# A dilation stage whose next rows are loaded ahead of the last rows' store and used one call later, and one PSUM bank copied by ScalarE

## The chip, the core and the metric

The kernel runs on one core of one Trainium2 chip. The metric is the device time of one launch in microseconds. Engines are named as the profile names them: PE is TensorE (PEld its weight loads), DVE is VectorE, ACT is ScalarE, POOL is GpSimd and SP is SyncE; the last two issue DMAs here and compute almost nothing. [...]

## What is computed

The input is 8 images of 8 channels of 256 x 256 in float32. Layer 0 of the reference is a Fourier operator (four rounds of spectral convolution plus 1x1 convolution, then a 1x1 convolution to 512 channels and one back to 8). Layer 1 is a dilation by a 3 x 3 square, padded by -2, of the normalized result. Both are added to their input:

```python
x = x + _L0_conv_ref(_gn(x), ...)
x = x + _L1_conv_ref(_gn(x))          # 3x3 maximum, border -2
```

## The kernel before, in words

**Three images are in work at once.** While image b goes through its four spectral layers (`layers`, L703), the two fully connected convolutions of image b-1 (its *head*, L789) are woven between them, and the dilation of image b-2 (its *tail*, `dilate`, L871) between those. The order on PE, DVE, ACT and SP is written out by hand: every stage is a generator that yields a string at the places where it lets others in. The loop at L938 reads the string: `f` is one step of the first convolution of a head (L825: 8 matmuls into four PSUM banks, then `act` by ACT at L826 and L827), `c` or `C` one of the second (L842: 16 matmuls, then a DVE addition at L851), and `t` one *call* of the oldest tail, that is, the dilation's code up to its next `yield`.

**A layer** handles the image in 11 chunks, two by two (k = 0 to 5). For each chunk `burst` (L593) makes 48 matmuls into four PSUM banks (L603 or L600, L606), which ACT evicts to `h` (L611, in layer 3 L613); DVE transposes the chunk in `turn` (L550); `transform` (L557) multiplies two chunks (L567) and DVE and ACT evict that (L574, L575); `gather` (L577) multiplies again (L585) and DVE evicts to `zt` (L588, L591). Where a pair has both chunks, k = 2 to 4 yields `ft`, then runs turn and transform, yields `t`, runs the second burst, yields `t`, and ends with `fc`. The last, single chunk (k = 5) yields `f`, then one `t`, then `fc`. Layer 3 has none of the turning; it yields `fct` eight times.

**Between two layers** stand the spectrum (`spectrum_h`, L375), the mixing on DVE (`mix`, L412) and, for the even layers, `rows_even` (L483). That one multiplies in three groups (`oi` = 0, 1, 2; L496) into PSUM banks `p_g`; group 0 has four banks, one in a buffer of one bank (`one`) and three in a buffer of three (`tri`), the other groups have three. There are two buffers of each kind, handed round in turn by all stages. `copy_banks` (L210) copies the banks to `zt`, by ACT (L215) those whose places are named in its second argument, by DVE (L217) the rest. In group 0 the banks are taken in the order 1, 2, 3, 0: the three of `tri` first. After image 0 (`alone[0]` false) groups 0 and 1 are copied by DVE alone, and of group 2 two banks by ACT.

**The dilation** of one image goes over 16 rows per partition in 8 groups of two rows. `yin` (one buffer, two rows and a row above and below), `m` and `o` (one buffer each) serve all groups. One group takes five calls:

- the last call of the group before ends with the store of `o` (L906) and, after the loop's turn, the load of `yin` (L878, 512 KB), both issued by POOL;
- a call that does nothing;
- the call that makes `m`, the maximum of neighbours (L889);
- the call that finishes it (L891), then the one that makes `o` (L894, L895);
- the call that normalizes `o`, sets the border and adds `yin` (L898 to L905), and then stores and loads as above.

The store waits for the addition L905; so does the load, which overwrites `yin`. `dilate` serves images 0 to 6; image 7 has its own stage (L747).

Of the kernel before, what the change touches and what calls it, by code (L numbers as in the profile page):

```python
# [39 lines left out]
DR = 2  # L40
# [6 lines left out]
def fno_dilate_kernel(ctx: ExitStack, tc: tile.TileContext, a: dict, out: bass.AP):  # L47
# [14 lines left out]
    def ps_tri(name):  # L62
        return ps.tile([128, 3, 512], F32, tag="tri", bufs=2, name=name)

    def ps_four(name):
        one, tri = ps_a(f"{name}_0"), ps_tri(f"{name}_1")
        return one, tri, [one] + [tri[:, i, :] for i in range(3)]

    def part(i):
        return slice(32 * i, 32 * i + 32)  # L70
# [137 lines left out]
    alone = [True]  # L208

    def copy_banks(pairs, by_act):  # L210

        done = []
        for i, (dst, src) in enumerate(pairs):
            if i in by_act:
                ins = nc.scalar.activation(dst, src, AF.Identity).ins  # L215
            else:
                ins = nc.vector.tensor_copy(dst, src).ins  # L217
            for other in done:
                if other.engine != ins.engine:
                    tc.declare_no_dep(ins, other, reason="two engines read banks of one tile and write apart")  # L220
            done.append(ins)
# [7 lines left out]
    def stats_end(st, name, out_):  # L229
        mv = sb.tile([128, 2], F32, tag="mv", name=f"mv_{name}")  # L230
        nc.vector.bn_aggr(mv, st.rearrange("p n s -> p (n s)"))
        yield
        yield
        p = corner(f"p_st_{name}")
        mm(p, grp, mv[:, 0:1], start=True, stop=True)
        if guest[0] is not None:
            yield
        mr = sb.tile([128, 2], F32, tag="mr", bufs=4, name=f"mr_{name}")
        nc.vector.tensor_copy(mr[:, 0:1], p)
        d = sb.tile([128, 1], F32, tag="d", name=f"d_{name}")  # L240
        nc.vector.tensor_tensor(d, mv[:, 0:1], mr[:, 0:1], ALU.subtract)
        nc.vector.scalar_tensor_tensor(mv[:, 1:2], d, d, mv[:, 1:2], ALU.mult, ALU.add)
        yield
        yield
        q = corner(f"p_sv_{name}")
        mm(q, grp, mv[:, 1:2], start=True, stop=True)
        if guest[0] is not None:
            yield


        v, r = mv[:, 0:1], mr[:, 1:2]
        nc.vector.tensor_scalar(v, q, EPS, None, ALU.add)
        rsqrt(v, r, d)
        yield
        out_["mr"] = mr
# [227 lines left out]
    def rows_even(b, l):  # L483

        zv = zt[:, :, :, : NBLK * WID].rearrange("p r f (n o) -> p o n f r", n=NBLK)
        n = NBLK * CS * NQ
        yield "ffc"
        for oi in range(NO):
            name = f"p_g_{b}_{l}_{oi}"
            if oi == 0:  # L490
                one, tri, banks = ps_four(name)
            else:
                tri = ps_tri(name)
                banks = [tri[:, r, :] for r in range(3)]
            for r, p in enumerate(banks):
                mm(p[:, :n], fz[part(r), oi].rearrange("p g k -> p (g k)"),  # L496
                   rowg[part(r), :, r % 2, :], start=True, stop=True)
            pairs = [(zv[:, NO * r + oi], banks[r][:, :n].rearrange("p (f n r) -> p n f r", n=NBLK, r=CS))
                     for r in ((1, 2, 3, 0) if oi == 0 else (0, 1, 2))]
            copy_banks(pairs, (0, 2) if oi == 2 else (1, 3) if alone[0] else ())  # L500
            yield "fcf"[oi]
        if l < 3:
            yield "t"
# [182 lines left out]
    def start(b, out_):  # L686
        if b < n_img:
            if b == 0:
                out_["sw"] = [load_sw(0, k) for k in range(3)]
            yield from spectrum_x(b, out_)  # L690
            yield from mix(b, 0, out_)
# [11 lines left out]
    def layers(b, stored, d, then, ahead):  # L703

        for l in range(4):
            if l > 0:
                yield from spectrum_h(b, l, d)  # L710
                yield from mix(b, l, d)
            yield from rows_odd(b, l, then) if l % 2 else rows_even(b, l)
            yield from layer(b, l, d, stored, then, ahead)
        yield "stored"
        yield from rest(b, then)
# [152 lines left out]
        return done, first, second, ahead  # L868


    def dilate(b, stats):  # L871
        d = {}
        yield from stats_end(stats, f"y{b}", d)
        mr = d["mr"]
        whole = y_rows[b % 2][:]
        o_rows = out[b].rearrange("c (p f) -> (c p) f", p=16)
        for r in range(0, 16, DR):
            nc.gpsimd.dma_start(  # L878
                yin[:, :, 1 : HW + 1],
                bass.AP(whole.tensor, whole.offset + r * HW, [[16 * HW, 128], [HW, DR + 2], [1, HW]]))  # L880
            yield
            yield

            if r == 0:
                nc.vector.tensor_scalar(yin[:, 0, :], yin[:, 0, :], edge[:, 0:1], None, ALU.min)
            if r == 16 - DR:
                nc.vector.tensor_scalar(yin[:, DR + 1, :], yin[:, DR + 1, :], edge[:, 1:2], None, ALU.min)
            m = sb.tile([128, DR + 2, HW], F32, tag="m", bufs=1, name=f"m_{b}_{r}")
            nc.vector.tensor_tensor(m, yin[:, :, 0:HW], yin[:, :, 1 : HW + 1], ALU.max)  # L889
            yield  # L890
            nc.vector.tensor_tensor(m, m, yin[:, :, 2 : HW + 2], ALU.max)  # L891
            yield
            o = sb.tile([128, DR, HW], F32, tag="o", bufs=1, name=f"o_{b}_{r}")
            nc.vector.tensor_tensor(o, m[:, 0:DR], m[:, 1 : DR + 1], ALU.max)  # L894
            nc.vector.tensor_tensor(o, o, m[:, 2 : DR + 2], ALU.max)  # L895
            yield

            nc.vector.tensor_scalar(o, o, mr[:, 0:1], mr[:, 1:2], ALU.subtract, ALU.mult)  # L898
            nc.vector.tensor_scalar(o[:, :, 0:1], o[:, :, 0:1], PAD, None, ALU.max)
            nc.vector.tensor_scalar(o[:, :, HW - 1 : HW], o[:, :, HW - 1 : HW], PAD, None, ALU.max)  # L900
            if r == 0:
                nc.vector.tensor_scalar(o[:, 0, :], o[:, 0, :], edge[:, 2:3], None, ALU.max)
            if r == 16 - DR:
                nc.vector.tensor_scalar(o[:, DR - 1, :], o[:, DR - 1, :], edge[:, 3:4], None, ALU.max)
            nc.vector.tensor_tensor(o, o, yin[:, 1 : DR + 1, 1 : HW + 1], ALU.add)  # L905
            nc.gpsimd.dma_start(o_rows[:, HW * r : HW * (r + DR)], o.rearrange("p r w -> p (r w)"))  # L906


# [17 lines left out]
    def tail():  # L926
        if tails and next(tails[0], tails) is tails:
            tails.pop(0)

    stats_of = {}  # L930
    with tc.manual_schedule(engines={PE, DVE, ACT, SP}):
        d = {}
        for _ in start(0, d):
            pass
        for b in range(n_img):
            stored = [dram.tile([128, NQ * PIX], F32, tag=f"hs{c}", name=f"stored_{b}_{c}") for c in range(NCH)]
            nxt, new, n_ready = {}, None, 0
            for n in layers(b, stored, d, start(b + 1, nxt), nxt):  # L938
                if n == "ready":
                    if new is None:  # L940
                        if b + 1 < n_img:
                            stats_of[b] = sb.tile([128, 8, 6], F32, tag="bn_y", name=f"bn_y{b}")
                        else:
                            stats_of[b] = spare[:, 16384:16480].rearrange("p (n s) -> p n s", s=6)
                        new = head(b, stored, stats_of[b])
                    new[3](n_ready)
                    n_ready += 1
                elif n == "stored":
                    heads.append((b, new))
                    alone[0] = False  # L950
                else:
                    for kind in n or "":
                        if kind == "t":
                            tail()
                        elif heads:
                            step(kind)
            d = nxt
        while heads:
            for kind in "ffc":
                if heads:  # L960
                    step(kind)
            tail()
        for t in tails:
            for _ in t:
                pass
# [170 lines left out]
```

## Time and profile before

| | |
|---|---|
| median of 3 runs | 3673.78 us (3665.64 to 3674.04) |
| the profiled execution | 3669.94 us, its span 3668.1 us |
| PE busy | 3478.0 us, 95% of the span |
| ACT busy | 2865.8 us, 78% |
| DVE busy | 2388.5 us, 65% |
| DVE waiting for `yin` before L889 | 26.1 us in 12 of 56 groups |
| mean granted PE clock | 0.979 |

Two views are read in what follows. The timeline shows instructions in order of time: start, duration, engine, line and operation, then in brackets how long the engine stood idle before it and what ended that. The list of waits adds these idle times up: who waited for whom, microseconds in all, how often, and the longest. Busy time is the sum over the whole span; PE's matmuls are pipelined, so 95% busy doesn't mean that 95% of the time PE could not have been faster.

### The profile page before, as it was taken

The page shows a single profiled execution, that of the slowest core. Times are in us where ns is not written, and L with a number is a line of the kernel's source. Part 1 is how long each engine was busy: PE and PEld are TensorE (multiplying, and loading weights), DVE is VectorE, ACT ScalarE, POOL GpSimd, SP SyncE. Part 2 cuts the span into 40 slices and gives each one's busy share as a digit, 9 for nine tenths or more (in the row PEclk, how much of TensorE's full clock was granted, in tenths as well). Part 3 has the DMA queues.
Part 4 walks back from the last instruction along what each step waited for, and adds up shares of the span by engine and source line. Part 5 has one row for each costly group of instructions (what it writes and reads, how often), then busy time and mean ns, then how long its engine had stood idle before and what let it go on. Part 6 is the DMA issues. An engine that isn't in the chain of part 4 may idle for free.

```text
span 3668.1 us, 112640 instructions
## 1 busy us (share of the span) xinstructions
PE 3478.0 (95%) x50872; PEld 1269.3 (35%) x50872; DVE 2388.5 (65%) x3711; ACT 2865.8 (78%) x3021; POOL 117.0 (3%) x202
## 2 busy tenths in 40 slices
PE   5768999999999999999999999999999999999997
PEld 2323333333333333333333333333333333333222
DVE  6776666557775677756776577766777567772443
ACT  2435888888788888787888888888878888879986
POOL 1000000000000000000000000000000000000000
PEclk7879999999999999999999999999999999999998
DMA  3006111442225312271214512253222531225221
GB/s 92 16 16 213 50 50 47 154 119 72 71 87 191 86 52 66 91 223 56 67 56 136 170 56 78 61 174 110 73 72 84 192 85 54 64 70 190 85 81 48
DMA packets 114081, 344.71 MB, mean 94 GB/s; under 512 B 15985, under 2 KB 18481, under 8 KB 98177
## 3 DMA queue, kind: packets, MB, share of 16 engines
q1 hardware_dynamic: 95392, 276.32, 24.8%
q0 software_dynamic: 18208, 61.18, 5.1%
q8 instruction: 400, 6.55, 0.7%
q14 instruction: 81, 0.66, 0.1%
HBM read 213.44 MB, written 123.74 MB: 92 GB/s over the span
## 4 chain that ended last, share of the span: by engine, by line
PE 74%; DVE 15%; issue 5%; ACT 4%; DMA 2%; POOL 0%; ACTq 0%; DVEq 0%; POOLq 0%
PE p_fc L842 20%; PE p_fc L825 20%; PE p_z L606 9%; PE p_d L567 7%; PE p_z L603 7%; PE p_z L600 3%; DVE turned L550 3%; PE p_u L585 3%; DVE y L851 3%; DVE S L423 2%; DVE turned L420 2%; DMA yin<-y_rows 2%; DVE turned L381 1%; PE p_g L518 1%; PE p_b L390 1%
## 5 line engine op out<-in xcount | busy, mean ns | idle before, releaser
L827 ACT ACTIVATE act<-p_fc 128x1536 f32<-128x1536 f32 x1024 | 1493.0, 1458 | 3.1 <-PE p_fc L825 3.1
L825 PE MATMUL p_fc<-hs,c_w 32*128 32x512 f32 x8192 | 1133.3, 626 | 29.8 <-DVE y L851 10.0
L842 PE MATMUL p_fc<-act,c_w 128*32 128x512 f32 x8192 | 1007.5, 599 | 0.2 <-ACT act L827 0.2
L826 ACT ACTIVATE act<-p_fc 128x512 f32<-128x512 f32 x1024 | 616.3, 602 | 214.1 <-PE p_fc L825 201.5
L550 DVE STREAM_TRANSPOSE turned<-h 128x1024 f32<-128x1024 f32 x528 | 632.4, 1225 | 179.0 <-ACT h L611 178.4
L611 ACT ACTIVATE h<-p_z 128x512 f32<-128x512 f32 (+1 forms) x528 | 511.9, 1021 | 205.0 <-PE p_z L606 204.9
L851 DVE TENSOR_TENSOR y<-p_fc,y 128x512 f32<-128x512 f32 x392 | 267.9, 683 | 524.9 <-PE p_fc L842 524.9
L825 PEld LDWEIGHTS p_fc<-hs,c_w 32*128 32x128 f32 x8192 | 356.6, 183 | 602.0 <-ACT act L826 259.2
L842 PEld LDWEIGHTS p_fc<-act,c_w 128*32 128x32 f32 x8192 | 222.5, 109 | 704.7 <-issue 330.7
L606 PE MATMUL p_z<-c_binv,zt 32*128 32x256 f32 x5632 | 410.4, 405 | 0.0
L606 PEld LDWEIGHTS p_z<-c_binv,zt 32*128 32x128 f32 x5632 | 259.3, 186 | 307.5 <-issue 294.4
L603 PE MATMUL p_z<-h,c_wt 32*32 32x512 f32 x8448 | 357.0, 602 | 7.9 <-ACT act L826 4.2
L567 PE MATMUL p_d<-turned,c_fw 32*32 32x480 f32 (+1 forms) x9216 | 308.9, 541 | 0.7 <-DVE turned L550 0.4
L575 ACT ACTIVATE turned<-p_d 128x1440 f32<-128x1440 f32 x144 | 182.9, 1270 | 90.9 <-PE p_d L567 87.6
L613 ACT ACTIVATE h<-p_z,c_bias 128x512 f32<-128x512 f32 (+1 forms) x176 | 186.5, 1110 | 71.7 <-PE p_z L606 71.5
L215 ACT ACTIVATE zt<-p_g 128x198 f32<-128x198 f32 (+2 forms) x118 | 53.6, 576 | 182.1 <-PE p_g L496 98.4
L423 DVE TENSOR_REDUCE S<-turned 128x80 f32<-128x800 f32 x192 | 189.0, 984 | 5.9
L420 DVE TENSOR_TENSOR turned<-t,B 128x800 f32<-128x800 f32 x192 | 188.7, 983 | 1.1
L567 PEld LDWEIGHTS p_d<-turned,c_fw 32*32 32x32 f32 x9216 | 127.3, 103 | 166.0 <-issue 65.0
L381 DVE STREAM_TRANSPOSE turned<-zt 128x960 f32<-128x960 f32 x96 | 177.2, 1873 | 2.5
L603 PEld LDWEIGHTS p_z<-h,c_wt 32*32 32x32 f32 x8448 | 93.2, 103 | 174.4 <-DVE y L851 48.8
L585 PE MATMUL p_u<-turned,c_stack 128*32 128x480 f32 (+1 forms) x1152 | 136.7, 543 | 11.5 <-DVE turned L574 6.2
(198 smaller groups left out, 1754.1 us busy)
## 6 DMA issues: line engine op xcount, KB each, us to landing
stored<-h SPq DMA_DIRECT2D x88, 1024.0 KB
hs<-stored SPq DMA_DIRECT2D x352, 256.0 KB
t<-in_spw SPq DMA_DIRECT2D x96, 400.0 KB
yin<-y_rows POOLq DMA_DIRECT2D x56, 512.0 KB, 5.1
h<-in_xp SPq DMA_DIRECT2D x352, 48.0 KB
turned<-in_xw SPq DMA_DIRECT2D x16, 1024.0 KB
y<-in_x SPq DMA_DIRECT2D x56, 256.0 KB
y_rows<-y POOLq DMA_DIRECT2D x56, 256.0 KB, 4.1
```

What stands on the lines that cost most here:

```text
L420: nc.vector.tensor_tensor(pr, sw[k], bt[:, k2, k].unsqueeze(2).to_broadcast([128, G, 2 * WID, WID]), ALU.mult)
L423: nc.vector.tensor_reduce(s[k2][:, k].rearrange("p s o g -> p (s o) g"), pr.rearrange("p g m i -> p m g i"), AX.X, ALU.add,)
L550: nc.vector.transpose(dst[:, 2 * i : 2 * i + 2], h[:, c, 2 * i : 2 * i + 2].rearrange("p f (s x) -> p f s x", s=2))
L567: mm(banks[q][part(v % 4), : 240 * n], fw8[part(q), v, :], t[part(q), :, :, v, : NBLK * WID], start=v < 4, stop=v >= 4)
L603: mm(o, wt[part(q), l, g, :], h[part(q), c, f, :], start=True, stop=False)
L606: mm(banks[q][:, HW * s : HW * (s + 1)], zt[part(q), 2 * c + s].rearrange("p f o -> p (f o)"), binv[part(q), :], start=False, stop=s == 1)
L611: nc.scalar.activation(dst, src, AF.Silu)
L825: mm(banks[g], w1[part(g), blk, :], hs[k][part(g), :], start=True, stop=True)
L826: nc.scalar.activation(act[:, 0, :], one, AF.Silu)
L827: nc.scalar.activation(act[:, 1:4, :], tri, AF.Silu)
L842: mm(acc[part(g), :], w2[:, g, 15 - rb - i : 47 - rb - i], act[:, g, :], start=i == 0, stop=i == 1)
L851: nc.vector.tensor_tensor(y, sums, y, ALU.add)
```

## The change

There are two edits. In the dilation, the load of the next two rows is issued in the call that finishes the last two, ahead of their store, and where that call came from the string `ft`, three calls instead of two pass between it and the use. In `rows_even`, ACT copies the first of group 0's banks (bank 1, of `tri`) instead of DVE; this is for images 1 to 7, layers 0 and 2.

```diff
-            copy_banks(pairs, (0, 2) if oi == 2 else (1, 3) if alone[0] else ())
+            copy_banks(pairs, (0, 2) if oi == 2 else (1, 3) if alone[0] else (0,) if oi == 0 else ())
...
+    close = [False]
...
-        for r in range(0, 16, DR):
+        def load_rows(r):
             nc.gpsimd.dma_start(
                 yin[:, :, 1 : HW + 1],
                 bass.AP(whole.tensor, whole.offset + r * HW, [[16 * HW, 128], [HW, DR + 2], [1, HW]]))
-            yield
-            yield
+        load_rows(0)
+        for r in range(0, 16, DR):
+            for _ in range(3 if close[0] else 2):
+                yield
...
             nc.vector.tensor_tensor(o, o, yin[:, 1 : DR + 1, 1 : HW + 1], ALU.add)
+            if r + DR < 16:
+                load_rows(r + DR)
             nc.gpsimd.dma_start(o_rows[:, HW * r : HW * (r + DR)], o.rearrange("p r w -> p (r w)"))
...
                 else:
+                    close[0] = n == "ft"
                     for kind in n or "":
```

## The prediction

> **What bounds the kernel now.** I read the page first, then the waits of DVE, then the timeline around the dilation's waits and around the row copies.
>
> ```profile
> PE 3478.0 (95%) x50872; PEld 1269.3 (35%) x50872; DVE 2388.5 (65%) x3711; ACT 2865.8 (78%) x3021; POOL 117.0 (3%) x202
> ...
> PE 74%; DVE 15%; issue 5%; ACT 4%; DMA 2%; POOL 0%; ACTq 0%; DVEq 0%; POOLq 0%
> ```
>
> PE sets the pace. Only what delays PE counts; DVE's 26.1 us of waiting for rows is not lost as such. In the waits of DVE and in the answer for the tile yin:
>
> ```profile
> DVE m L889 <- DMA yin<-y_rows: 26.1, 12, 3.3
> ```
> ```profile
> DMA to landing us min/median/max: 4.3/5.4/9.1
> ```
>
> The 12 waits are two in each of images 0 to 5, at rows 6 and rows 12. By the trace the rows 6 waits are 1.63, 1.18, 1.47, 1.24, 1.39, 1.54 us (sum 8.45) and the rows 12 waits 2.58, 3.33, 2.74, 3.12, 2.98, 2.92 us (sum 17.67). What they cost PE is read from the timeline's distance between equal steps. Rows 6 of image 1, in layer 1:
>
> ```profile
> 1366.57 2.19 PE L567 MATMUL p_d<-turned,c_fw 32*32 32x480 f32 x58
> ...
> 1372.26 0.54 POOL L906 DMA_DIRECT2D out<-o  x1 [23.55 <-DVE o L905]
> ...
> 1372.79 0.76 POOL L878 DMA_DIRECT2D yin<-y_rows  x1
> ...
> 1377.82 2.19 PE L567 MATMUL p_d<-turned,c_fw 32*32 32x480 f32 x58
> ...
> 1378.73 1.22 DVE L889 TENSOR_TENSOR m<-yin 128x1024 f32<-128x1024 f32 x1 [1.18 <-DMA yin<-y_rows]
> ...
> 1389.93 2.29 PE L567 MATMUL p_d<-turned,c_fw 32*32 32x480 f32 x64
> ```
>
> Undisturbed, a pair of chunks takes 11.25 us (1366.57 to 1377.82); with the wait 12.11. Measured at ACT's eviction of the chunks, the six such pairs take 12.56, 12.12, 12.40, 12.17, 12.32, 12.47 us: 1.31 + 0.87 + 1.15 + 0.92 + 1.07 + 1.22 = **6.5 us** lost. Each is its wait less 0.32, so DVE has 0.32 us of slack there.
>
> For rows 12 I take the way from the last eviction of layer 2 to the first of layer 3. ACT's timeline, image 1 of the spectral layers (no dilation runs yet) above image 3:
>
> ```profile
> 631.41 1.94 ACT L611 ACTIVATE h<-p_z 128x512 f32<-128x512 f32 x2 [1.10 <-PE p_z L606]
> ...
> 690.25 2.12 ACT L613 ACTIVATE h<-p_z,c_bias 128x512 f32<-128x512 f32 x2 [0.36 <-PE p_z L606]
> ...
> 1499.28 1.94 ACT L611 ACTIVATE h<-p_z 128x512 f32<-128x512 f32 x2 [1.10 <-PE p_z L606]
> ...
> 1559.31 2.12 ACT L613 ACTIVATE h<-p_z,c_bias 128x512 f32<-128x512 f32 x2 [0.36 <-PE p_z L606]
> ```
>
> 58.84 against 60.03 us. Over images 2 to 7 the excess is 0.36 + 1.20 + 0.61 + 1.00 + 0.84 + 0.79 = **4.8 us**: each wait less about 2.1 us of slack.
>
> The row copies, layer 0 of image 3:
>
> ```profile
> 1214.23 1.95 DVE L217 COPY zt<-p_g 128x264 f32<-128x264 f32 x4
> 1214.32 0.31 PEld L825 LDWEIGHTS p_fc<-hs,c_w 32*128 32x128 f32 x8 [0.57 <-DVE y L851]
> 1214.32 1.14 PE L825 MATMUL p_fc<-hs,c_w 32*128 32x512 f32 x8 [0.16 <-DVE y L851]
> 1215.54 0.60 ACT L826 ACTIVATE act<-p_fc 128x512 f32<-128x512 f32 x1 [1.41 <-PE p_fc L825]
> ...
> 1215.88 0.72 PE L496 MATMUL p_g<-c_rowg,fz 32*128 32x264 f32 x6 [0.41 <-DVE zt L217]
> ```
>
> Group 1's matmuls need the tri buffer that DVE's third copy frees (1215.73). PE stands idle 0.41 us, while ACT has been idle for 1.41.
>
> **What the Trainium skill says.** *DMA: Bandwidth & Descriptors*, "Anatomy of one DMA — SWDGE (gpsimd) path", gives a fit of 2.0 us plus bytes / 436e3 per us: an estimate of 3.2 us for these 512 KB. The trace shows 4.3 to 9.1, so I use the trace. The same page, "Queues, rings and completion order", says that a completion increment lands only after every earlier write of that DMA engine. A load queued behind a store therefore also waits for the store's bytes. The trace shows little of it while the queues are quiet: in image 6 the first load, with no store directly ahead, lands after 4.53 us, the next two, with one, after 4.56 and 5.14. *PSUM — Partial Sum Buffer*, "Specifications (TRN2)", says that ScalarE and VectorE read PSUM in parallel if their banks differ. The trace agrees: in group 2 an ACT and a DVE copy start together at 1219.16 and take 0.66 and 0.65 us.
>
> **The change, part by part.**
>
> *Rows 12, a call later.* Only these six groups come from `ft` (k = 4 of layer 2); all others finish in a plain `t` or in `fct`. Their L889 moves to the one `t` of k = 5, some 8 us later (L891 stood there: 1505.23 against 1497.29), long after the landing at 1497.27. The wait is gone: **-4.8 us**. L891 to L905 of this group and everything of the last group shift by one `fct` of layer 3. This fits: the eighth `fct` only found an ended generator before. DVE's work there is unchanged but for place, and layer 3's chunks keep one rhythm in image 1 without a dilation and in images 2 to 6 with one (12.97, 12.97, 14.57, 13.70, 12.48 us per two chunks), so cost nothing; without that slack it would be at most one call, 1.6 us, in six images, 9 us. The moved load of rows 14 now has a call at about 1584 instead of 1571. There it took 7.4 us and was used 4.5 us after landing; it keeps two calls.
>
> *Load ahead of the store.* POOL's issue of the store takes 0.54 us, so the load starts 0.53 us sooner, and its 512 KB no longer follow the store's 256. On rows 6 the loads take 5.9 to 6.4 us since SP loads (hs) share the engines. I take 0.75 us sooner; the bounds are 0.53 (the issue alone) and 1.2 (the store's bytes as well: 64 packets of some 0.17 us on 16 engines, 0.7 us). With 0.75 the loss left is (wait - 0.75 - 0.32) = 0.56 + 0.11 + 0.40 + 0.17 + 0.32 + 0.47 = 2.0 of 6.5: **-4.5 us** (3.2 to 6.4). All other groups had their rows in time. The store comes 0.76 us later behind the load on POOL's queue; its only customer is the next L894, at least 8.0 us after the old landing. If that cover went, each late us would hit DVE.
>
> *ACT's copy.* Fourteen copies of 0.65 us, 9 us of ACT. In layer 0 it fits in the 1.41 us idle (1214.2 to 1214.9); DVE's two other tri banks are done at 1215.29, so group 1 starts at the end of p_fc, 1215.46: PE gains its idle time, 0.42 + 0.41 + 0.43 + 0.43 + 0.41 + 0.43 in images 2 to 7, 0.05 in image 1. In layer 2 ACT's L827 ends later and PE was idle only 0.09: seven times that is 0.6. **-3.2 us** (1.5 to 3.5). The added wait stands ahead of `act` L826, which waits for PE anyway until 0.3 us after the copy's end in layer 2; if ACT were late, p_fc's buffers and PE would be behind it.
>
> *Sum:* -4.8 - 4.5 - 3.2 = **-12.5 us**, bounds -8.8 to -14.7 (the lower with rows 12 at 4.1). Against the profiled 3669.94 that gives 3657.4; against the median of the runs, 3.84 us higher, 3661.3. I forecast between them, **3660 us**.
>
> **The rivals.**
>
> 1. *The load lands no sooner.* On rows 6 its time is set by the SP loads and the memory, not by its place. For it: 5.9 to 6.4 us there against 4.3 to 5.0 at rows 2, 4 and 10, all behind a store. Against: the issue alone is 0.53. Then -4.8 - 3.2 = -8.0: 3665 us, too small to tell.
> 2. *ACT's copy comes late.* It waits for a DVE and a PE count. If it ran only after DVE's three copies (1215.7), it would end at 1216.4: tri is freed 0.65 us later than now and L826 starts 0.84 later. About 0.8 x 14 = 11 us, less the loads' 9.3: +2, 3675 us, and slower as soon as the delay passes 0.66 us each. Against: the copy is first in program order, and group 2's ACT copies start together with DVE's.
> 3. *The copies gain nothing,* because a later DVE or ACT step takes the 0.4 us back: -9.3, 3663 us.
>
> **How the numbers follow.** A measurement of this kernel can tell about 0.3%, 11 us, from no change; its runs spread over 8.4. Likeliest case 0.66, rival 1 0.18, rival 3 0.09, rival 2 0.07. The forecast lies 1.5 us beyond the bound, so I give faster 0.60 and within 0.35; slower 0.05, rival 2 with a longer delay than the one priced. The range runs from the lowest run less 14.7 (3651) to the highest less 8 (3666), 1 to 2 us wider for the clock: three stretches of 3.4 us at half clock cost 1.6 us each, and they come as they like.
>
> **What would show it.** After: no wait of L889 at rows 12, six shorter ones at rows 6 (0.4 to 0.9 us); the last pair of layer 1 at 11.4 to 11.8 us and layer 2 to 3 at 58.9; L215 beside L217 in group 0 and no idle PE before L496. It is wrong if layer 3's rhythm lengthens, if new waits stand before L894 or the rows 14 use, or if L826 starts later after its PE step.

## The result, and the profile after

The changed kernel takes 3657.48 us (median of 6 runs, 3651.77 to 3659.54), the kernel before 3671.65 us in the same measurement (6 runs, 3665.64 to 3674.04). The ratio is 0.9961 with a 95% interval of 0.9951 to 0.9971: 14.3 us faster, between 10.6 and 18.0. The forecast was 3660 us and 12.5 us faster. On another chip the same kernel gave 0.9950 (0.9936 to 0.9963).

The profiled execution took 3659.15 us, its span 3657.4 us. First the page: engine times, then the chain of work that ended last.

```profile
PE 3478.5 (95%) x50872; PEld 1271.2 (35%) x50872; DVE 2381.7 (65%) x3697; ACT 2873.7 (79%) x3035; POOL 117.0 (3%) x202
...
PE 80%; DVE 13%; ACT 4%; issue 3%; DMA 0%; ACTq 0%; DVEq 0%; POOL 0%; POOLq 0%
```

PE was and is busy 95% of the time; what changed is the chain. DMA has gone from it (2% before) and PE's share is up from 74% to 80%. DVE's waits say the same (waiter, line, releaser: microseconds in all, times, longest):

```profile
DVE m L895 <- DMA yin<-y_rows: 0.8, 3, 0.4
```

26.1 us in 12 groups became 0.8 us in 3 (L895 is the old L889). Rows 6 of image 1 in the timeline:

```profile
1367.24 2.19 PE L567 MATMUL p_d<-turned,c_fw 32*32 32x480 f32 x58
...
1378.49 2.19 PE L567 MATMUL p_d<-turned,c_fw 32*32 32x480 f32 x58
...
1389.72 2.29 PE L567 MATMUL p_d<-turned,c_fw 32*32 32x480 f32 x64
```
```profile
1372.93 0.76 POOL L881 DMA_DIRECT2D yin<-y_rows  x1 [23.55 <-DVE o L911]
1373.68 0.54 POOL L914 DMA_DIRECT2D out<-o  x1
```

The load now goes out first, and the last pair of layer 1 takes 11.23 us like the one before it, in place of 12.11. The way from layer 2 to layer 3, in ACT's timeline (image 3 again):

```profile
1498.66 1.94 ACT L611 ACTIVATE h<-p_z 128x512 f32<-128x512 f32 x2 [1.10 <-PE p_z L606]
...
1557.56 2.12 ACT L613 ACTIVATE h<-p_z,c_bias 128x512 f32<-128x512 f32 x2 [0.36 <-PE p_z L606]
```

58.90 us instead of 60.03. The row copies, layer 0 of image 3:

```profile
1212.89 0.73 PE L496 MATMUL p_g<-c_rowg,fz 32*128 32x264 f32 x8
...
1213.68 0.62 ACT L215 ACTIVATE zt<-p_g 128x264 f32<-128x264 f32 x1
1213.75 1.51 DVE L217 COPY zt<-p_g 128x264 f32<-128x264 f32 x3
1213.77 0.31 PEld L825 LDWEIGHTS p_fc<-hs,c_w 32*128 32x128 f32 x8 [0.57 <-DVE y L851]
1213.77 1.14 PE L825 MATMUL p_fc<-hs,c_w 32*128 32x512 f32 x8 [0.16 <-DVE y L851]
...
1214.95 0.72 PE L496 MATMUL p_g<-c_rowg,fz 32*128 32x264 f32 x6
1214.99 0.60 ACT L826 ACTIVATE act<-p_fc 128x512 f32<-128x512 f32 x1 [0.69 <-PE p_fc L825]
```

ACT's copy runs beside DVE's three. Group 1's matmuls (the second L496) start 2.06 us after those of group 0 (the first), and `act` L826 still waits for PE. Before, group 1 started at 1215.88 and group 0 here, 2.44 us earlier:

```profile
1213.44 0.73 PE L496 MATMUL p_g<-c_rowg,fz 32*128 32x264 f32 x8
```

Where the time went, by the distances between equal steps over images 1 to 7 (from one to another of ACT's second, larger evictions of a chunk, so that single values differ by 0.1 us from the timeline's rows, which begin with the first):

| stretch | before | after | gain |
|---|---|---|---|
| last pair of layer 1 (rows 6), six times | 12.12 to 12.56 | 11.24 | 6.6 us |
| layer 2 to layer 3 (rows 12), six times | 59.29 to 60.13 | 58.88 to 59.11 | 4.6 us |
| layer 3 to the next layer 0 (copy), 0.34 + 6 x 0.38 | 31.15 (27.53 once) | 30.77 (27.19) | 2.6 us |
| layer 1 to layer 2 (copy), seven times | 58.90 | 58.54 | 2.5 us |
| sum | | | 16.3 us |

The two spans differ by only 10.7. What is missing lies in the first two chunks of layer 0, and it is the clock. Busy times and clock of that step in two executions: the kernel before, images 2 and 4,

```profile
788.70:797.00 8.30, 8.30 (x159) 3.32 (x129) 5.34 (x5) 7.69 (x10) 0.00 (x0) 1.00 0.13 33
1657.70:1667.60 9.90, 9.90 (x160) 4.05 (x129) 5.34 (x5) 7.70 (x10) 0.00 (x0) 0.83 0.10 28
```

and the changed kernel, image 2:

```profile
788.70:798.50 9.80, 9.80 (x160) 4.03 (x129) 5.34 (x5) 7.65 (x10) 0.00 (x0) 0.83 0.10 28
```

The columns after the length are PE, PEld, DVE, ACT and POOL busy, the granted PE clock, and DMA. The same instructions take 9.8 us at a mean clock of 0.83 and 8.3 at 1.00: a stretch of 3.4 us at half clock. The profile of before has it in two of the images 2 to 7, that of after in all six: 4 x 1.55 = 6.2 us, which leaves 16.3 - 6.2 = 10.1. The other 0.6 us is the net of three parts that no experiment followed: after the change, image 0 takes 0.8 us longer, image 1's way from layer 2 to layer 3 takes 0.3 us longer, and what comes after the last layer 1.6 us less.

### The profile page after: what moved, and what is told of

The parts are those of the page before. It is cut to its first block, busy times and chain, and to the rows that moved or that the text cites. A ratio compares the mean times of both kernels' runs of the same rounds, so it can differ in the third digit from the quotient of the medians.

```text
span 3657.4 us, 112630 instructions
## 1 busy us (share of the span) xinstructions
PE 3478.5 (95%) x50872; PEld 1271.2 (35%) x50872; DVE 2381.7 (65%) x3697; ACT 2873.7 (79%) x3035; POOL 117.0 (3%) x202
## 4 chain that ended last, share of the span: by engine, by line
PE 80%; DVE 13%; ACT 4%; issue 3%; DMA 0%; ACTq 0%; DVEq 0%; POOL 0%; POOLq 0%
PE p_fc L825 21%; PE p_fc L842 21%; PE p_z L606 10%; PE p_d L567 8%; PE p_z L603 8%; PE p_u L585 3%; PE p_z L600 3%; DVE y L851 2%; DVE S L423 2%; DVE turned L420 2%; DVE turned L550 2%; PE p_b L390 1%; DVE turned L381 1%; PE p_g L518 1%; ACT act L826 1%
## 5 line engine op out<-in xcount | busy, mean ns | idle before, releaser
L825 PE MATMUL p_fc<-hs,c_w 32*128 32x512 f32 x8192 | 1132.7, 625 | 24.6 <-DVE y L851 10.0
L826 ACT ACTIVATE act<-p_fc 128x512 f32<-128x512 f32 x1024 | 616.0, 602 | 199.7 <-PE p_fc L825 187.6
L825 PEld LDWEIGHTS p_fc<-hs,c_w 32*128 32x128 f32 x8192 | 357.9, 184 | 595.0 <-ACT act L826 260.2
L215 ACT ACTIVATE zt<-p_g 128x198 f32<-128x198 f32 (+2 forms) x132 | 62.5, 583 | 177.6 <-PE p_g L496 93.7
```

The costliest lines, as they stand in the source:

```text
L825: mm(banks[g], w1[part(g), blk, :], hs[k][part(g), :], start=True, stop=True)
L826: nc.scalar.activation(act[:, 0, :], one, AF.Silu)
```

## The experiments

A gain with an interval is (1 - ratio) times the median of before in the same measurement, 3671.05 us for the first four experiments and 3673.45 for the next four. "The distances" are those of the table above, read from each profile.

**The ACT copy alone.** In `rows_even` of the kernel before:

```diff
-            copy_banks(pairs, (0, 2) if oi == 2 else (1, 3) if alone[0] else ())
+            copy_banks(pairs, (0, 2) if oi == 2 else (1, 3) if alone[0] else (0,) if oi == 0 else ())
```

> The row copy alone. By the trace of the changed kernel, the way from layer 3 to the next layer 0 is 0.38 us shorter (31.15 to 30.77) and from layer 1 to layer 2 0.36 us (58.90 to 58.54), seven times each: 2.6 + 2.5 = 5.1 us faster, not the 3.2 of the prediction, whose layer 2 had 0.09 a time. The changed kernel's profile also shows a stretch of half PE clock, 3.4 us long, at the first bursts of layer 0 in all of images 2 to 7, where before had it in two of them; each makes that step 1.55 us longer. Theory: the copy in layer 0, which closes PE's last idle gap before these bursts, brings these stretches. Then this profile has them in all six images too, and the net gain is about 5.1 - 4 x 1.55 = -1 us, no faster than before. Rival: they come by chance or from the dilation edit; then few of them here and about 5 us faster.

Measured 0.9988 (0.9981 to 0.9994): 4.4 us faster, 2.2 to 7.0. Both distances of the copy shrink as in the changed kernel, by 5.1 us in sum. Stretches of half clock appear in images 2 and 5 only, and the mean clock of these 21 runs is that of the 42 runs of before, 0.979. So the copy is worth about 5 us, and my idea that it brings the stretches falls. The dilation's twelve waits remain (26.1 us before):

```profile
DVE m L889 <- DMA yin<-y_rows: 28.7, 12, 3.6
```

They are 2.6 us longer in this profile, nearly all of it at rows 12, whose loads landed 6.14 us after the addition on the mean (5.75 before); the way from layer 2 to layer 3 is 2.4 us longer in sum, so that all distances together give 2.6 us here. Whether that is the copy's doing or the loads' own spread, one profile does not show; in the kernels with the load ahead, the profiles with the copy and those without it differ by at most 0.2 us in this landing, in both directions.

**The load ahead of the store alone.** From the changed kernel:

```diff
-            for _ in range(3 if close[0] else 2):
+            for _ in range(2):
...
-            copy_banks(pairs, (0, 2) if oi == 2 else (1, 3) if alone[0] else (0,) if oi == 0 else ())
+            copy_banks(pairs, (0, 2) if oi == 2 else (1, 3) if alone[0] else ())
```

> The load ahead of the store alone, two calls as before, no copy. The rows 6 loads came 1.2 to 1.6 us sooner after the addition in the changed kernel, so theory: rows 12 waits fall from 2.6 to 3.3 us to about 1.4 to 2.1, under the 2.1 us of slack there, and the later call adds nothing: 6.5 + 4.8 = 11.3 us faster. Rival, as the prediction had it: rows 12 needs the later call; with 0.75 us sooner, 0.75 x 6 = 4.5 of rows 12's waits go but at most some 3.5 of its 4.8 us, so 9 to 10 us faster, with the way from layer 2 to layer 3 still 0.2 to 0.5 us above 58.9.

Measured 0.9969 (0.9958 to 0.9980): 11.4 us faster, 7.3 to 15.4. Of that, some 3 us is the clock: at the runs' clock of 0.980 it averages 3659.2 us (4 runs) against 3667.5 (5 runs) of before, 8.3 us. The distances give 6.6 us at rows 6 and 1.5 at rows 12. DVE's waits:

```profile
DVE m L895 <- DMA yin<-y_rows: 17.1, 9, 3.2
```

and its timeline at rows 12 of image 2, the addition, then the use:

```profile
1922.07 0.69 DVE L911 TENSOR_TENSOR o<-o,yin 128x512 f32<-128x512 f32 x1
...
1928.79 1.23 DVE L895 TENSOR_TENSOR m<-yin 128x1024 f32<-128x1024 f32 x1 [3.20 <-DMA yin<-y_rows]
```

Rows 12 still wait 2.4 to 3.2 us. The load is issued 0.3 us after the addition instead of 0.87, yet lands 5.54 us after it on the mean, against 5.75 (more profiles of both orders stand below the last table). My theory (the later call adds nothing) falls; the rival, that of the prediction, is nearer, and even it expected more at rows 12.

**The later call alone.** The load behind the store, as before, but with the third call, and no copy:

```diff
-            if r + DR < 16:
-                load_rows(r + DR)
             nc.gpsimd.dma_start(o_rows[:, HW * r : HW * (r + DR)], o.rearrange("p r w -> p (r w)"))
+            if r + DR < 16:
+                load_rows(r + DR)
```

> The later call alone: the load is still issued in the finishing call but behind the store, no copy. Both theories: rows 12 don't wait (4.8 us faster), rows 6 wait as before (1.2 to 1.6 us) and the last pair of layer 1 stays at 12.1 to 12.6 us. About 5 us faster. If it is worth nothing, what rows 12 lost was not its wait.

Measured 0.9983 (0.9977 to 0.9990): 6.2 us faster, 3.7 to 8.4. DVE's waits, and ACT's way from layer 2 to layer 3 in image 3:

```profile
DVE m L895 <- DMA yin<-y_rows: 7.7, 6, 1.6
```
```profile
1501.68 1.94 ACT L611 ACTIVATE h<-p_z 128x512 f32<-128x512 f32 x2 [1.10 <-PE p_z L606]
...
1560.53 2.12 ACT L613 ACTIVATE h<-p_z,c_bias 128x512 f32<-128x512 f32 x2 [0.36 <-PE p_z L606]
```

The six waits at rows 6 are left (the pair at 12.02 to 12.54 us), those of rows 12 are gone: 58.85 us by these rows, and by the distances 58.94 in all six images. So 4.7 us belong to the later call. The pairs at rows 6, which no edit touches here, are 0.7 us shorter in sum than before: so much the landings differ from one profile to another.

**The load ahead, and the copy in layer 2 only.** The load-ahead kernel with this:

```diff
-            copy_banks(pairs, (0, 2) if oi == 2 else (1, 3) if alone[0] else ())
+            copy_banks(pairs, (0, 2) if oi == 2 else (1, 3) if alone[0] else (0,) if oi == 0 and l == 2 else ())
```

> The load ahead of the store, two calls as before, and the ACT copy in layer 2 only. Theory (the layer 0 copy brings the stretches of half clock, the later call adds nothing): 11.3 + 2.5 = 13.8 us faster, two or three stretches in layer 0 at most, and no slower than the changed kernel, perhaps some 3 us faster than it. Rival (stretches have nothing to do with the layer 0 copy): they come here as often as in the changed kernel, and it is 2.6 us slower than that one.

Measured 0.9969 (0.9956 to 0.9981): 11.4 us faster, 7.0 to 16.2. Layer 1 to layer 2 takes 58.52 us on the mean, so layer 2's copy gives its 2.6 us by itself. Rows 12 wait as in the load-ahead kernel (2.5 to 3.2 us), and the sum by the distances is 6.6 + 0.9 + 2.6 = 10 us. The measured gain is no larger than that of the load ahead alone, but those runs had the higher clock: compared with runs of before at their own clock, these are 10.8 us faster at 0.979 (3 runs) and 11.7 at 0.978 (2 runs), against 8.3 there. Stretches of half clock: two in layer 0.

**No store behind the load.** The load-ahead kernel, without the stores of groups 2 to 14 of images 0 to 6:

```diff
+            if r == 0:
-            nc.gpsimd.dma_start(o_rows[:, HW * r : HW * (r + DR)], o.rearrange("p r w -> p (r w)"))
+                nc.gpsimd.dma_start(o_rows[:, HW * r : HW * (r + DR)], o.rearrange("p r w -> p (r w)"))
```

> Two calls as before, no ACT copy, the load as in the changed kernel, and no store behind it: the rows of groups 2 to 14 of images 0 to 6 are not written to the output (the first group of each image is). With the load alone ahead of the store, rows 12 still landed 5.2 to 6.0 us after the addition (before: 5.4 to 6.1), though it was issued 0.53 us sooner. Theory: the store's bytes, moved between the last of the load's, hold it back by about what the sooner issue gains; without them rows 12 land 4.6 to 5.0 us after the addition and wait 1.7 to 2.2 us instead of 2.4 to 3.2. Rival: the load's own slow start (some 2 us with packets of 0.3 to 0.5 us) sets the landing; then rows 12 land 5.2 to 6.0 us after the addition as with the store. The time says nothing about a kernel that writes everything.

Rows 12 landed 4.85 to 5.76 us after the addition, 5.34 on the mean (5.54 with the store), and waited 2.0 to 3.0 us:

```profile
DVE m L895 <- DMA yin<-y_rows: 15.2, 6, 3.0
```

Neither range: the store's bytes cost the load 0.2 us there, and the greater part is the load's own time. Elsewhere the theory came nearer: without the store behind it, rows 6 land at 4.91 us instead of 5.52 and rows 10 at 4.50 instead of 5.09, so a store *behind* the load costs it up to 0.6 us. The packets' records show what it is made of. In the load-ahead kernel, rows 12 of image 1, POOL's queue moves 11, 17, 24 and 21 packets in the four half microseconds from 1.5 us after the addition, at 0.22 to 0.46 us each, and then 48 per half microsecond at 0.16. With the store ahead, 56 packets go at 0.17 us each between 1.0 and 2.0 us, while the load is not yet under way; then follows the load's slow start, 7, 17, 27 and 25 packets. At rows 12, a store ahead moves in time in which the load's own bytes do not yet move.

**The dilation's two edits, then with the copy in layer 2, then all.** The changed kernel without the ACT copy; with it only where `l == 2`; and unchanged.

> Both dilation edits, no ACT copy. Theory (the parts add): rows 6 gives 6.5 us and rows 12 4.7 us, 11.2 us faster; it differs from the load alone by the 1.5 us that rows 12 still lost there. Rival: the edits get in each other's way in layer 3, where everything of the last group shifts by a call; then layer 3's rhythm (12.97, 12.97, 14.57, 13.70, 12.48 us) is longer somewhere and the gain under 9 us.

> The changed kernel with the ACT copy in layer 2 only. Theory: 11.2 + 2.5 = 13.7 us faster than before, 2.6 slower than the changed kernel. Rival (the layer 0 copy brings stretches of half clock in that kernel, although it did not when it stood alone): as fast as the changed kernel or faster, with a higher mean clock over the runs.

> The changed kernel once more, on the chip of its parts. Theory: 6.5 + 4.7 + 5.1 = 16.3 us faster than before where both have as many stretches of half clock; six stretches in layer 0 instead of two, as in its first profile, would make it 10. If the six were chance, this profile has one to three and a span near 3652 us; if they belong to the kernel, six again and 3657.

| kernel | ratio | faster by | by the distances | stretches in layer 0 |
|---|---|---|---|---|
| both dilation edits | 0.9965 (0.9952 to 0.9977) | 12.9 us | 11.2 us | 3 |
| with the copy in layer 2 | 0.9953 (0.9941 to 0.9966) | 17.3 us | 14.0 us | 3 |
| all | 0.9950 (0.9936 to 0.9963) | 18.4 us | 16.2 us | 2 |

The parts add: each sum by the distances lies within its measured interval, though the steps from one kernel to the next are smaller than these intervals. Layer 3's rhythm is 12.97, 12.97, 14.57, 13.70, 12.48 us in all three, to 0.01 us, so the shift by a call costs nothing there. The changed kernel's second profile has two stretches and a span of 3652.8 us: so the six of the first need not come with the kernel. Whether chance or the other chip brought them is open. No version measured here is faster than the changed kernel.

**Where the sooner landing at rows 6 comes from.** First a quarter of the store ahead of the load and the rest behind it, then the store and a second one of the same size (to a scratch tensor) ahead of it; both with two calls and without the copy:

```diff
+            flat = o.rearrange("p r w -> p (r w)")
+            nc.gpsimd.dma_start(o_rows[:, HW * r : HW * r + 128], flat[:, 0:128])
             if r + DR < 16:
                 load_rows(r + DR)
+            nc.gpsimd.dma_start(o_rows[:, HW * r + 128 : HW * (r + DR)], flat[:, 128:])
-            nc.gpsimd.dma_start(o_rows[:, HW * r : HW * (r + DR)], o.rearrange("p r w -> p (r w)"))
```
```diff
+        copy_of = dram.tile([128, DR * HW], F32, tag="copy_of", name=f"copy_of_{b}")
...
+            nc.gpsimd.dma_start(o_rows[:, HW * r : HW * (r + DR)], o.rearrange("p r w -> p (r w)"))
+            nc.gpsimd.dma_start(copy_of, o.rearrange("p r w -> p (r w)"))
             if r + DR < 16:
                 load_rows(r + DR)
-            nc.gpsimd.dma_start(o_rows[:, HW * r : HW * (r + DR)], o.rearrange("p r w -> p (r w)"))
```

> Two calls as before, no ACT copy. A quarter of the store (64 of 256 KB) is issued ahead of the load, the rest behind it: the load is issued as late as before, with fewer bytes ahead. What is read is the time from the addition L905 to the landing of rows 6 and rows 12 (before: 7.0 and 5.75 us on the mean; with the load ahead of the whole store 5.5 and 5.5). Theory (at rows 6 the bytes ahead matter most, since they wait behind the SP load and the load's slow start comes after them): rows 6 at 6.0 us, that is 5.5 plus the 0.53 of the issue; rows 12 at 5.7. Rival (only the place in the queue counts, however little stands ahead): rows 6 at 6.7 to 7.0.

> Two calls as before, no ACT copy, the store ahead of the load as in the kernel before, and after it a second store of the same 256 KB to a scratch tensor, also ahead of the load: the suspected cost twice. Theory (issue 0.53 and bytes): the load is issued 1.36 us after the addition instead of 0.83; rows 6 land at 7.0 + 0.53 + 0.7 = 8.2 us, rows 12 at 6.3 to 7.0. Rival (bytes ahead of the load cost nothing, only the issue does): rows 6 at 7.5, rows 12 at 6.3. The kernel is slower than before either way, by about the longer waits less nothing: rows 6 and 12 lose 0.5 to 1.2 us each in six images, 6 to 14 us.

From the addition to the landing, mean of six images:

| ahead of the load | load issued | rows 6 | rows 12 |
|---|---|---|---|
| nothing, and no store behind it | 0.30 us | 4.91 us | 5.34 us |
| nothing, the store behind it | 0.30 | 5.52 | 5.54 |
| 64 KB, the rest behind it | 0.82 | 6.37 | 5.78 |
| 256 KB (before) | 0.83 to 0.87 | 6.97 | 5.75 |
| 2 x 256 KB | 1.39 to 1.40 | 7.43 | 6.95 |

One row is one profile, and the landings differ between profiles. With the whole store ahead, the means of three profiles are 6.85 to 6.99 us at rows 6 and 5.73 to 6.14 at rows 12; with the load ahead of it, those of six are 5.42 to 5.52 and 5.40 to 5.62. So going first is worth 1.45 us at rows 6 and some 0.4 at rows 12 on the mean of all, 0.2 in the two profiles of the table.

Rows 6, a quarter ahead: 6.37 lies between the theory's 6.0 and the rival's 6.7. Against 5.52, 0.85 us come with the later issue and the first 64 KB, and 0.60 with the other 192 KB. The second store costs rows 6 only 0.46, about its issue (the rival's reading), but rows 12 1.20, issue and bytes (the theory's). So bytes ahead don't have one price; by the packets' records they cost where the load could otherwise have moved. The kernel with a quarter ahead ran 3671.97 us against 3671.30 of before, one run each, though its pairs at rows 6 are 3.5 us shorter in sum; its profile has two stretches of 6.8 us at half clock, which cost 3.2 us more than those in the profile of before. DVE's waits grow as they should in the kernel with two stores:

```profile
DVE m L896 <- DMA yin<-y_rows: 41.8, 22, 4.5
```

That kernel ran 3691.14 us against 3671.30, one run each, 19.8 us slower where I expected 6 to 14. The two expected distances lose 2.8 and 9.9 us more than before, 12.7 and so within what I expected; rows 10, which I had left out, waits 4.2 us too and makes layer 2 longer by 2.8 us in sum, and its profile has more stretches of half clock (3.2 us more in layer 0). I did not divide the rest.

## Why the prediction was right

- **Rows 12, a call later:** -4.8 forecast, 4.6 by the distances; by itself 4.7 by the distances and 6.2 (3.7 to 8.4) measured. Right, in mechanism and size; the shift in layer 3 is free, as argued from the equal rhythm of image 1.
- **Load ahead of the store:** -4.5 forecast, 6.6 found. The mechanism held: rows 6 land sooner. But the term "I take 0.75 us sooner" was too small, and its upper bound of 1.2 too: rows 6 land 1.45 us sooner. I had added the issue (0.53) and the store's bytes (0.7), as if bytes behind the load cost nothing (they cost 0.6 us here), but not that the load's slow start then runs while the SP load is still moving. In the load-ahead kernel at rows 6 of image 1, POOL's slow packets and SP's run together from 1.5 to 3.5 us after the addition; with the store ahead the slow start began when SP's were through. That this overlap makes up the difference fits the records but was not isolated. At rows 12 the same edit gives 0.2 us in this pair of profiles and some 0.4 over all, less than the 0.53 I took as the least; the later call hid that error.
- **ACT's copy:** -3.2 forecast, 5.1 by the distances, 4.4 (2.2 to 7.0) by itself. Layer 0 was right in its sum only (2.6 forecast and found): images 2 to 7 gave 0.38 each, for 0.41 to 0.43 forecast, and image 1 gave 0.34, for 0.05. The term "in layer 2 [...] PE was idle only 0.09" failed: the gain there is 0.35 a time. Before, layer 2 of image 3:

```profile
1437.73 0.73 PE L496 MATMUL p_g<-c_rowg,fz 32*128 32x264 f32 x8
...
1438.53 1.96 DVE L217 COPY zt<-p_g 128x264 f32<-128x264 f32 x4
1438.61 0.65 PEld L825 LDWEIGHTS p_fc<-hs,c_w 32*128 32x128 f32 x8 [0.57 <-DVE y L851]
1438.61 1.48 PE L825 MATMUL p_fc<-hs,c_w 32*128 32x512 f32 x8 [0.16 <-DVE y L851]
...
1440.18 0.72 PE L496 MATMUL p_g<-c_rowg,fz 32*128 32x264 f32 x6
```

and after:

```profile
1437.50 0.73 PE L496 MATMUL p_g<-c_rowg,fz 32*128 32x264 f32 x8
...
1438.29 1.51 DVE L217 COPY zt<-p_g 128x264 f32<-128x264 f32 x3
1438.38 0.65 PEld L825 LDWEIGHTS p_fc<-hs,c_w 32*128 32x128 f32 x8 [0.57 <-DVE y L851]
1438.38 1.48 PE L825 MATMUL p_fc<-hs,c_w 32*128 32x512 f32 x8 [0.16 <-DVE y L851]
1438.53 0.65 ACT L215 ACTIVATE zt<-p_g 128x264 f32<-128x264 f32 x1
...
1439.50 0.80 PE L496 MATMUL p_g<-c_rowg,fz 32*128 32x264 f32 x6
```

  Here L496 starts at 1439.50, while the page lets L825 end at 1438.38 + 1.48 = 1439.86. An end of a matmul is modelled; I took it for the moment from which PE was free. The starts of L496 tell more: before, group 1 started 0.15 us after the end of DVE's third copy in layer 0 and in layer 2 alike (1215.73 and 1440.03), 2.44 and 2.45 us after group 0; after, 2.06 and 2.00. Read by that distance, both layers had the same wait, and so had image 1 in layer 0 (2.45, then 2.07).
- **Sum:** 12.5 against 16.3 by the distances, both misses to the low side. The first measurement, 14.3, lies between. In its profile four more stretches of half clock than before took back 6.2 us; the clock of its six runs (0.977 to 0.979) makes it likely that such stretches lengthened its other runs too, but the clocks of the runs of before beside them are not on record. That the measured time came within 3 us of 3660 is therefore partly luck.
- **The rivals.** That the load lands no sooner is wrong for rows 6, and not far off for rows 12. ACT's copy does not come late: it starts at 1213.68, DVE's at 1213.75. No later step takes its gain back.

## What to carry to other kernels

Price a wait by the distance between equal steps of the engine that sets the pace, with the wait and without it, rather than by the idle time of the engine that waits: here 26.1 us of DVE's idle time were worth 11.2. Read what releases a matmul from starts, not from its predecessor's modelled end. When a transfer is late for its use, moving the use by more than the wait takes the whole wait away, where the work can be shifted (rows 12, in all six images). What moving the transfer ahead in its queue gives depends on the other traffic of that moment: 1.45 us at rows 6 and some 0.4 at rows 12 for the same edit.

## What the runs showed of the hardware that was not expected

- From image 1 to the end of the last image's layers, stretches of 3.4 us at half PE clock (6.8 us in four of all cases) fall on the first bursts of layer 0, in one to six images of a profile; only the kernel with two stores has two elsewhere. Each short one costs 1.55 us. Time and clock go together from run to run. On the chip of the first experiments the kernel before ran 3673.3 us on the mean at a clock of 0.978 (18 runs), 3669.9 at 0.979 (19) and 3667.5 at 0.980 (5), so a difference of a few microseconds is best read at equal clock. What sets the stretches off stays open; the experiments tie them to none of the edits.
- A load of 512 KB by POOL's queue starts slowly: at rows 12 of image 1 its 4 KB packets take 0.2 to 0.5 us for about 2 us, then 0.16. Why was not tried.
- Whether a store of 256 KB stands ahead of that load or behind it, it can cost the load time: taken away altogether, rows 6 land 0.6 us sooner than with it behind and 2.1 sooner than with it ahead, rows 12 only 0.2 and 0.4.
